# A four-layer graph network on one core: decoding and norm steps reordered in layer 0, inverse roots moved between layers 1 and 2

## The chip, the cores and the metric

The kernel runs on one core of a Trainium2 chip. The core has a matrix engine (TensorE, "PE" in the profile, with weight loads as "PEld"), three engines for elementwise work (VectorE or "DVE", ScalarE or "ACT", GpSimd or "POOL"), and SyncE ("SP"), which here only issues DMA transfers. Each engine runs its own instructions strictly in order, and engines wait for each other through semaphores. The metric is the time of one execution on the device in microseconds (us); lower is better.

## The reference

x has 2708 rows (nodes) of 512 features. adj is a 2708 x 2708 matrix that is almost empty: each entry is nonzero with probability 0.0015, plus the diagonal, with values in 0.05 to 1. Four layers follow one another, each of the form x = layernorm(x + layer(x, adj)):

```python
# layer 0
e2 = (adj @ x) * (diag + 1);        y = (x - e2) @ W + bias
# layer 1
h = x @ W_sa
scores = (h @ a_left)[:, None] + (h @ a_right)[None, :]
e = where(adj != 0, exp(-leaky_relu(scores, 0.01)), 0)
x_a = (e / (e.sum(1) + 1e-5)) @ h;  x_b = adj @ (x @ W_gcn) + b_gcn
y = sigmoid(gate_a * x_a + gate_b * x_b)      # gates: sigmoids of linear forms of adj @ x and x
# layer 2
mask = adj > 0;  inc = adj + mask / sqrt(mask.sum(1));  y = (inc @ x) / inc.sum(1)
# layer 3
A = adj + I;  d = A.sum(0) ** -0.5;  y = tanh((d[:, None] * A * d[None, :]) @ x @ W.T + b)
```

## The kernel before

**Lists instead of a dense matrix.** The 2708 rows are cut into NB = 24 blocks of R = 113 (the last has 109). For each block the kernel makes a list of up to 512 edges (four chunks of 128), and a product with adj becomes four products of a small matrix (128 edges by 113 rows) with 128 gathered rows of 512 features. The function `gather` (line 600) fetches those rows by four indirect DMAs that POOL issues; `aggregate` (L613) is the four products on PE. Layer 0 builds the lists as it goes; layers 1 to 3 use them again, gathering from tables in device memory that the layer before wrote.

**The order is written by hand** (`manual_schedule`): each engine executes its instructions in the order in which the code calls them. All direct loads and stores are issued from SP's single queue, in the order of the calls.

**Layer 0.** Blocks of 113 rows carry the aggregation, windows of 128 rows (KB = 22 of them) carry the products with the weights. Before the loop the first three blocks are searched, with some unread products (`keep_busy`, L797) placed on PE. Then 26 steps, k = 0 to 25, do the following, with m = k+2 the block whose list is decoded:

- `turn_x` transposes the last window's normalised rows (PE), `ranges`, `mark`, `fetch` (L901 to L913) decode block m's list: `starts` (L889 to L896: a PE product and three ACT instructions that make "ahead", "middle", "q") has been issued in the step before, `mark` compares q on DVE, and `fetch` is eight PE products.
- `project0` (o_l) multiplies a window by w0. In step k=1, two products `times_a` (L827), part of preparing layer 1's score weights, stand ahead of it; `score_rows` and `score_columns` copy and turn their result.
- `negatives` (L845) is an ACT pass over a whole adjacency block. `search` finds the eight largest values of one of four segments of a block, and their places (DVE, L858 and L860); after the fourth segment `count` (L872 to L882) sums up and the load of a later adjacency block is issued on SP. A step searches `parts` segments: 4, or 5 ahead of a step without a window, or fewer in and behind such a step.
- `pick` (L922 to L956) turns the fetched list into indices, row numbers and values, issues the gather of block m, and ends with an ACT instruction for `nvalue`. `values0(m)` makes the block's edge matrix with eight ACT instructions (L966, L967); `sums0(m)` (l0a) multiplies it in the step after.
- `load_window` loads a window of x on SP into one of two tiles `xw`, one step before `bias0` adds the bias to it (DVE, L990). `residual0` adds the projection (DVE L1000) and has three ACT instructions for the variance, the last a square root (L1009).
- `norm0` has a DVE reciprocal (L1017) and two ACT instructions (L1018, L1019) that write the normalised rows.
- `next0` (h) and `rest0` (hb) multiply the window before by layer 1's weights; `next0` ends in four ACT copies and the stores of `to_blocks`. `inputs0` (DVE, L979 to L984) and `turn_u` (L1064, L1073) prepare the next aggregated block.

Windows and blocks do not match, so steps 8 and 17 have no window ("bare"), and steps 9 and 18 follow them (`parts` = 3). The order at the end of a step before the change:

```python
                pick(m)
                own[m] = load_own(m)
...
                residual0(w)
...
            if w is not None:
                norm0(w)
            if wx is not None and not bare:
                next0(wx)
            if m < NB:
                values0(m)
            search(parts - 3)
            if k + 1 < NB:
                sums0(k + 1)
                inputs0(k + 1)
```

**Layer 1 and the way to layer 2.** In block i, `sums1` and `scored_sums1` are PE products, `gates1` and `gated1` work on the first, `both1`, `stats1` and `norm1` finish block i-1; `norm1` stores the block to table 1. `source_sums_in` brings column sums of adj into `deg` with a PE transpose and an ACT copy. `row_norms` (L1540 to L1545) makes inverse square roots of row counts with a power on POOL; `d_inv` (L1638) is another such power. `keep_warm(12)` (L1530) puts unread products on PE, and `spread_bias(b3_bc)` (L1504, L1505) broadcasts a bias row with a PE product and a DVE copy. Layer 2 starts with the gathers of blocks 0 and 1 from table 1 and with `incidence` (L1567, L1570), which makes the edge matrix `s_left` of a block on DVE.

**Layer 2 and the way to layer 3.** Per block: four gathers, four products (l2a), one unread product, statistics, and `norm2`, which writes the normalised rows `xr` and then `y`, which is xr scaled by d_inv, each with one ACT pass (L1689, L1693); y is stored to table 2, from which layer 3 gathers.

Of the kernel before, what the change touches and what calls it, by code (L numbers as in the profile page):

```python
# [447 lines left out]
def sparse_stack(  # L448
# [199 lines left out]
    with ExitStack() as phase:  # L648
# [106 lines left out]
        load_diagonal(0, 4, R)  # L755
        nc.sync.dma_start(out=w0_sb, in_=w0.rearrange("(b p) o -> p b o", p=P))
        own[1] = load_own(1)


        nc.gpsimd.iota(  # L760
# [385 lines left out]
        count(1)  # L1146
        starts(1)
        values0(0)
        keep_busy(2)
        find(2, (0,), places=False)  # L1150
        ranges(1)
        mark(1)
# [14 lines left out]
        load_adj(5)  # L1167
        count(2)
        sums0(0)
        starts(2)  # L1170
        gate_columns()
        turn_w(0)
# [33 lines left out]
        for k in range(NB + 2):  # L1206
            m = k + 2
            w, wx, rest = window_at.get(k), window_at.get(k - 1), window_at.get(k - 1)
            bare = 2 < k < NB and w is None
            after = 2 < k < NB and wx is None  # L1210
            parts = 4
            if any(t not in window_at for t in (k + 1, k + 2, k + 3)) and 2 < k < NB - 4:
                parts = 5
            if bare:
                parts, rest = 2, None
            if after:
                parts, rest = 3, window_at[k - 2]
            if wx is not None and k <= NB:
                turn_x(wx)
            if m < NB:  # L1220
                ranges(m)
                mark(m)
                fetch(m)
            if k == 1:
                times_a(2)
                times_a(3)
            if w is not None:
                project0(w)
            if k == 0:
                times_a(0)  # L1230
                turn_w(2)
            if unstored:
                store0(unstored.pop())
            if k + 3 < NB:
                negatives(k + 3)
            if k == 1:
                score_rows()
            search(1)
            if m < NB:
                pick(m)  # L1240
                own[m] = load_own(m)
            if w is not None:
                bias0(w)
            search(1)
            if w is not None:
                residual0(w)
            if k + 1 in window_at:
                load_window(window_at[k + 1])
            if parts > 2:
                search(1)  # L1250
            if w is not None:
                norm0(w)
            if wx is not None and not bare:
                next0(wx)
            if m < NB:
                values0(m)
            search(parts - 3)
            if k + 1 < NB:
                sums0(k + 1)
                inputs0(k + 1)  # L1260
            if k == 1:
                score_columns()
            if k + 2 == NB:
                worst = check_lists()
                for i in range(4):
# [232 lines left out]
    bg_bc = gpool.tile([P, D], FP, name="bg_bc")  # L1498
    nc.sync.dma_start(out=bg_bc[0:1, :], in_=b_gc[None, :])

    def spread_bias(t):
        ps = ps_sp.tile([P, 4, P], FP, tag="sp", name="bias_rows")
        ps = ps.rearrange("p k r -> p (k r)")
        nc.tensor.matmul(ps, lhsT=one_row, rhs=t[0:1, :], start=True, stop=True)  # L1504
        nc.vector.tensor_copy(t, ps)  # L1505
# [13 lines left out]
    def source_sums_in():  # L1519
        ps = ps_sp.tile([P, 4, P], FP, tag="sp", name="deg_s")  # L1520
        nc.tensor.transpose(ps[:R, 0, :NB], deg_r, ident[:NB, :NB])
        nc.scalar.copy(deg[:R, :], ps[:R, 0, :NB])

    def keep_warm(pool, tag, shape, n, cols=D):

# [11 lines left out]
    def row_norms(at):  # L1537
        n = at.stop - at.start

        nc.vector.tensor_scalar(  # L1540
            cnt[:, at], cnt[:, at], 2.0**23, 2.0**23, op0=ALU.add, op1=ALU.subtract
        )
        nc.vector.tensor_add(cnt[:, at], cnt[:, at], plus[:, at])
        nc.vector.tensor_scalar(inv_norm[:, at], cnt[:, at], 1e-24, None, op0=ALU.max)
        nc.gpsimd.tensor_tensor(  # L1545
            inv_norm[:, at], inv_norm[:, at], root.to_broadcast([P, n]), ALU.pow
        )

    row_in, inc2 = {}, {}

# [33 lines left out]
    for i in range(NB):  # L1584
# [41 lines left out]
    nc.vector.tensor_mul(plus, plus, inv_norm)  # L1626
    nc.vector.tensor_add(plus, plus, adiag)
    nc.vector.tensor_mul(cnt, cnt, inv_norm)
    nc.vector.tensor_add(rowsum, rowsum, cnt)
# [7 lines left out]
    nc.vector.tensor_add(d_inv, deg, zero)  # L1637
    nc.gpsimd.tensor_tensor(d_inv, d_inv, root.to_broadcast([P, NB]), ALU.pow)  # L1638
# [43 lines left out]
    def norm2(i):  # L1682
        r = rows(i)
        v, mv = v2.pop(i)
        nc.vector.reciprocal(mv[:r, 2:3], mv[:r, 2:3])
        nc.vector.tensor_scalar(
            mv[:r, 3:4], mv[:r, 0:1], mv[:r, 2:3], -1.0, op0=ALU.mult, op1=ALU.mult
        )
        nc.scalar.activation(  # L1689
            xr[:r, i, :], v[:r, :], AF.Identity, bias=mv[:r, 3:4], scale=mv[:r, 2:3]  # L1690
        )
        y = spool.tile([P, D], FP, tag="y", name=f"y2_{i}")
        nc.scalar.activation(y[:r, :], xr[:r, i, :], AF.Copy, scale=d_inv[:r, i : i + 1])  # L1693
        move_rows(r, lambda a, b: table[2][i * R + a : i * R + b, :], lambda a, b: y[a:b, :])

    own2(0)
# [149 lines left out]
```

## Time and profile before

| | us |
|---|---|
| median of 3 runs | 988.07 |
| lowest and highest run | 983.52, 988.93 |
| the profiled execution: its time | 1001.58 |
| its span, first to last instruction | 999.7 |

| busy in the profiled span | us | share |
|---|---|---|
| PE | 898.5 | 90% |
| PE weight loads | 498.5 | 50% |
| DVE | 685.7 | 69% |
| ACT | 527.9 | 53% |
| POOL | 472.4 | 47% |

The mean granted TensorE clock is 0.954. The stages, read from the timeline: the first 62 us are the start of layer 0, whose loop runs to about 419; layer 1 from there to 632, layer 2 from about 653 to 789, layer 3 from about 800 to the end. In a timeline each line gives start, length, engine, source line, operation, output<-inputs, shapes and count, and in brackets how long the engine had been idle before and what released it. A line of the source can be a helper's, so that one line stands for many tiles. One fp32 product appears as two PE records.

### The profile page before, as it was taken

The page shows a single profiled execution, that of the slowest core. Times are in us where ns is not written, and L with a number is a line of the kernel's source. Part 1 is how long each engine was busy: PE and PEld are TensorE (multiplying, and loading weights), DVE is VectorE, ACT ScalarE, POOL GpSimd, SP SyncE. Part 2 cuts the span into 40 slices and gives each one's busy share as a digit, 9 for nine tenths or more (in the row PEclk, how much of TensorE's full clock was granted, in tenths as well). Part 3 has the DMA queues.
Part 4 walks back from the last instruction along what each step waited for, and adds up shares of the span by engine and source line. Part 5 has one row for each costly group of instructions (what it writes and reads, how often), then busy time and mean ns, then how long its engine had stood idle before and what let it go on. Part 6 is the DMA issues. An engine that isn't in the chain of part 4 may idle for free.

```text
span 999.7 us, 11191 instructions
## 1 busy us (share of the span) xinstructions
PE 898.5 (90%) x2963; PEld 498.5 (50%) x2963; DVE 685.7 (69%) x1803; ACT 527.9 (53%) x1220; POOL 472.4 (47%) x538
## 2 busy tenths in 40 slices
PE   6789999899998999988888879887797889999994
PEld 2445656455654655466666667432332334444441
DVE  7877889787997743168888789586586525555543
ACT  5857677577677563357776667243354412222222
POOL 3322323323323220066666665576777375767640
PEclk8879999999999899989999999989898998999997
DMA  9976877787876444389999996266666464555531
GB/s 244 304 206 188 241 213 228 224 227 207 240 209 194 141 120 144 103 300 299 313 292 315 294 290 224 85 191 192 201 207 199 123 174 139 162 168 152 174 107 35
DMA packets 133516, 201.70 MB, mean 202 GB/s; under 512 B 82456, under 2 KB 82502, under 8 KB 133445
## 3 DMA queue, kind: packets, MB, share of 16 engines
q0 software_dynamic: 36864, 111.73, 37.4%
q1 hardware_dynamic: 96581, 89.18, 31.3%
q8 instruction: 26, 0.43, 0.2%
q14 instruction: 45, 0.37, 0.1%
HBM read 181.83 MB, written 27.80 MB: 210 GB/s over the span
## 4 chain that ended last, share of the span: by engine, by line
PE 66%; DVE 11%; DMA 9%; issue 4%; ACT 3%; POOL 3%; another core or an unknown queue 2%; SPq 1%; POOLq 0%; DVEq 0%; ACTq 0%
PE o_l L584 15%; PE l3a L613 9%; PE l2a L613 8%; PE hb L584 7%; PE h L584 7%; DMA gath<-table,source 7%; PE l0a L613 6%; PE unread L1530 3%; PE l1s L1407 3%; POOL gath L600 2%; PE fetched L913 2%; PE l1e L1417 2%; DVE where_all L860 2%; DMA gath<-in_x_dram 1%
## 5 line engine op out<-in xcount | busy, mean ns | idle before, releaser
L600 POOL DMA_INDIRECT gath<-table,source x288 | 314.6, 1093 | 164.9 <-issue 79.7
L600 POOL DMA_INDIRECT gath<-in_x_dram,source x96 | 97.8, 1019 | 233.7 <-issue 204.3
L1407 PE MATMUL l1s<-gath,s 128*113 128x256 f32 (+3 forms) x384 | 93.6, 398 | 23.9 <-DVE l1b L1437 23.4
L613 PE MATMUL l2a<-gath,s_left 128*113 128x512 f32 (+1 forms) x192 | 93.5, 629 | 3.5 <-DVE s_left L1570 2.0
L613 PE MATMUL l3a<-gath,s 128*113 128x512 f32 (+1 forms) x192 | 90.4, 614 | 3.6 <-DMA gath<-table,source 3.6
L1407 PEld LDWEIGHTS l1s<-gath,s 128*113 128x113 f32 (+1 forms) x384 | 68.7, 184 | 49.5 <-DVE l1b L1437 32.2
L1417 PE MATMUL l1e<-gath,e 128*113 128x257 f32 (+3 forms) x384 | 87.0, 379 | 0.2 <-issue 0.2
L613 PE MATMUL l0a<-gath,s 128*113 128x512 f32 (+1 forms) x192 | 86.9, 593 | 0.2 <-DMA gath<-in_x_dram,source 0.2
L584 PE MATMUL o_l<-shared,uT_l 128*113 128x512 f32 (+1 forms) x192 | 86.4, 592 | 0.7 <-ACT uT_l L577 0.7
L584 PE MATMUL hb<-w_gc_sb,uT_x 128*128 128x512 f32 (+1 forms) x176 | 83.3, 601 | 0.0
L584 PE MATMUL o_l<-w_sb,uw 128*128 128x512 f32 (+1 forms) x176 | 82.9, 615 | 0.2
L584 PE MATMUL h<-w_sa_sb,uT_x 128*128 128x259 f32 (+1 forms) x352 | 80.8, 382 | 0.0
L1417 PEld LDWEIGHTS l1e<-gath,e 128*113 128x113 f32 (+1 forms) x384 | 68.0, 177 | 15.7 <-issue 0.6
L584 PEld LDWEIGHTS h<-w_sa_sb,uT_x 128*128 128x128 f32 (+1 forms) x352 | 64.8, 185 | 19.8 <-issue 6.6
L1530 PE MATMUL unread<-bg_bc,ident 128*128 128x512 f32 x88 | 47.1, 655 | 21.9 <-remote 17.2
L1765 ACT ACTIVATE y<-l3v,mv_l 113x512 f32<-113x512 f32 (+1 forms) x24 | 19.5, 813 | 81.9 <-DVE mv_l L1761 74.4
L613 PEld LDWEIGHTS l2a<-gath,s_left 128*113 128x113 f32 (+1 forms) x192 | 34.4, 191 | 53.3 <-issue 44.5
L584 PEld LDWEIGHTS o_l<-shared,uT_l 128*113 128x113 f32 (+1 forms) x192 | 34.0, 177 | 48.7 <-issue 47.7
L1739 DVE SCALAR_TENSOR_TENSOR l3v<-o_l,d_inv,b_bc 113x512 f32<-113x512 f32 (+1 forms) x25 | 18.1, 729 | 58.5 <-PE o_l L584 55.1
L613 PEld LDWEIGHTS l3a<-gath,s 128*113 128x113 f32 (+1 forms) x192 | 33.3, 184 | 43.5 <-issue 39.4
L613 PEld LDWEIGHTS l0a<-gath,s 128*113 128x113 f32 (+1 forms) x192 | 33.5, 177 | 39.9 <-issue 35.3
L1294 DVE TENSOR_SCALAR s<-niota_r,nrow,edges 128x113 f32<-128x113 f32 x192 | 51.3, 342 | 0.0
(239 smaller groups left out, 1594.1 us busy)
## 6 DMA issues: line engine op xcount, KB each, us to landing
shared<-in_adj_dram SPq DMA_DIRECT2D x14, 1186.5 KB
table<-st SPq DMA_DIRECT2D x21, 514.5 KB
gath<-in_adj_dram SPq DMA_DIRECT2D x7, 1186.5 KB
shared<-table SPq DMA_DIRECT2D x16, 448.0 KB
gath<-in_x_dram SPq DMA_DIRECT2D x21, 256.0 KB
xi<-in_x_dram SPq DMA_DIRECT2D x23, 224.0 KB
table<-xr SPq DMA_DIRECT2D x23, 224.0 KB
table<-y SPq DMA_DIRECT2D x23, 224.0 KB
```

Of the source, the lines that this page charges most:

```text
L584: nc.tensor.matmul(o, lhsT=uT[:, f, :r], rhs=w[:, f, :], start=(f == 0), stop=(f == DB - 1))
L600: nc.gpsimd.indirect_dma_start(out=g[:, c, :n], out_offset=None, in_=src[:, :], in_offset=bass.IndirectOffsetOnAxis(ap=source[:, i, c : c ...
L613: nc.tensor.matmul(agg[:r, :], lhsT=s[:, c, :r], rhs=g[:, c, off : off + D], start=(c == 0), stop=(c == EC - 1),)
L860: nc.vector.max_index(out=where_all[:, i, g * 8 : (g + 1) * 8], in_max=top, in_values=seg)
L913: nc.tensor.matmul(t["fetched"][:, c, : 3 * NS], lhsT=t["q"][:, c * P : (c + 1) * P], rhs=rec_all[:, i].rearrange("p k s -> p (k s)"), sta ...
L1294: nc.vector.tensor_scalar(s[:, c, :], niota_r, nrow[:, i, c : c + 1], edges[:, i, c, 1:2], op0=ALU.is_equal, op1=ALU.mult,)
L1407: nc.tensor.matmul(sum_s[i][:r, k, : at.stop - at.start], lhsT=s[:, c, :r], rhs=g[:, c, at], start=(c == 0), stop=(c == EC - 1),)
L1417: nc.tensor.matmul(sum_e[i][:r, k, k : k + at.stop - at.start], lhsT=e[:, c, :r], rhs=g[:, c, at], start=(c == 0), stop=(c == EC - 1),)
L1530: nc.tensor.matmul(o[:, :cols], lhsT=ident, rhs=bg_bc[:, :cols], start=True, stop=True)
L1739: nc.vector.scalar_tensor_tensor(v[:r, at], o[:r, at], d_inv[:r, i : i + 1], b3_bc[:r, at], op0=ALU.mult, op1=ALU.add,)
L1765: nc.scalar.activation(y[:r, :], v[:r, :], AF.Identity, bias=mv[:r, 3:4], scale=mv[:r, 2:3])
```

## The change

In layer 0, the first two windows of x are loaded right behind block 1's own rows, ahead of adjacency block 3 and the later weights on SP's queue, and are no longer loaded in the loop. One of the two unread products before `fetch(1)` is taken away, and two are added behind `sums0(0)`. In a step, `project0` comes before `times_a(2)` and `times_a(3)`; `values0(m)` comes right behind `pick(m)` and `load_own(m)`, ahead of `bias0`; the last searches of a step are put together; `next0` comes before `norm0`, which is last. In step k=1 `score_rows` moves behind `values0`.

From layer 1 to layer 2: in the last iteration the statistics of block 22 come after `gated1(23)`; `source_sums_in` runs after the last `norm1`, and its copy is DVE's; the bias row's product goes out behind `both1(23)`, and the copy follows later; the incidence work of blocks 0 and 1 comes before the gathers; `d_inv` and the last two columns of `row_norms` use a square root on ACT and a reciprocal on DVE instead of POOL's power; the unread products fall from 12 to 8; the sums over `rowsum`, `plus` and `cnt` come behind the gathers' calls. In `norm2` of the last block y is made from v with a combined scale and bias, ahead of xr.

```diff
         own[1] = load_own(1)
+        load_window(0)
+        load_window(1)
...
-        keep_busy(2)
+        keep_busy(1)
         find(2, (0,), places=False)
...
         sums0(0)
+        keep_busy(2)
         starts(2)
...
+            if w is not None:
+                project0(w)
             if k == 1:
                 times_a(2)
                 times_a(3)
-            if w is not None:
-                project0(w)
...
-            if k == 1:
-                score_rows()
             search(1)
             if m < NB:
                 pick(m)
                 own[m] = load_own(m)
+                values0(m)
+            if k == 1:
+                score_rows()
...
-            if k + 1 in window_at:
+            if window_at.get(k + 1, 0) > 1:
                 load_window(window_at[k + 1])
-            if parts > 2:
-                search(1)
+            search(parts - 2)
+            if wx is not None and not bare:
+                next0(wx)
             if w is not None:
                 norm0(w)
-            if wx is not None and not bare:
-                next0(wx)
-            if m < NB:
-                values0(m)
-            search(parts - 3)
...
+    def spread_row(t, name):
+        ps = ps_sp.tile([P, 4, P], FP, tag="sp", name=f"rows_{name}")
+        spread_ps[name] = ps = ps.rearrange("p k r -> p (k r)")
+        nc.tensor.matmul(ps, lhsT=one_row, rhs=t[0:1, :], start=True, stop=True)
...
-        nc.gpsimd.tensor_tensor(
-            inv_norm[:, at], inv_norm[:, at], root.to_broadcast([P, n]), ALU.pow
-        )
+        if on_pool:
+            nc.gpsimd.tensor_tensor(
+                inv_norm[:, at], inv_norm[:, at], root.to_broadcast([P, n]), ALU.pow
+            )
+        else:
+            nc.scalar.sqrt(inv_norm[:, at], inv_norm[:, at])
+            nc.vector.reciprocal(inv_norm[:, at], inv_norm[:, at])
...
         if i + 1 == NB:
-            source_sums_in()
             turn_norm(0)
             turn_norm(1)
...
-        if i > 0:
+        if 0 < i < NB - 1:
             stats1(i - 1)
...
         if i + 1 < NB:
             mask1(i + 1)
+        else:
+            stats1(i - 1)
...
-    row_norms(slice(KB, NB))
     copy_norm(0)
     copy_norm(1)
-    keep_warm(ps_sp, "sp", [P, 4, P], 12)
+    keep_warm(ps_sp, "sp", [P, 4, P], 8)
     both1(NB - 1)
+    spread_row(b3_bc, "b3")
     stats1(NB - 1)
-    nc.vector.tensor_add(rowsum, rowsum, adiag)
...
     norm1(NB - 1)
+    deg_ps = source_sums_in()
+    inc_s = [values(0)]
+    incidence(0, inc_s[0])
+    inc_s.append(values(1))
+    incidence(1, inc_s[1])
+    nc.vector.tensor_copy(b3_bc, spread_ps["b3"])
+
+    nc.vector.tensor_copy(deg[:R, :], deg_ps[:R, 0, :NB])
...
-    nc.gpsimd.tensor_tensor(d_inv, d_inv, root.to_broadcast([P, NB]), ALU.pow)
-    spread_bias(b3_bc)
+    nc.scalar.sqrt(d_inv, d_inv)
+    row_norms(slice(KB, NB), False)
...
     for i in range(2):
         gather(gath[i], i, table[1], D)
-        incidence(i, values(i))
+    nc.vector.tensor_add(rowsum, rowsum, adiag)
...
+    nc.vector.reciprocal(d_inv, d_inv)
     nc.vector.reciprocal(rowsum, rowsum)
...
+        if i + 1 == NB:
+
+            di = d_inv[:r, i : i + 1]
+            nc.vector.tensor_mul(mv[:r, 0:2], mv[:r, 2:4], di.to_broadcast([r, 2]))
+            nc.scalar.activation(
+                y[:r, :], v[:r, :], AF.Identity, bias=mv[:r, 1:2], scale=mv[:r, 0:1]
+            )
```

More of the change, by code (lines that the diff above doesn't have):

```diff
@@ L1499, in sparse_stack @@
     nc.sync.dma_start(out=bg_bc[0:1, :], in_=b_gc[None, :])
+    spread_ps = {}
+    def spread_row(t, name):
+        ps = ps_sp.tile([P, 4, P], FP, tag="sp", name=f"rows_{name}")
+        spread_ps[name] = ps = ps.rearrange("p k r -> p (k r)")
+        nc.tensor.matmul(ps, lhsT=one_row, rhs=t[0:1, :], start=True, stop=True)
     def spread_bias(t):
@@ L1521, in source_sums_in @@
         nc.tensor.transpose(ps[:R, 0, :NB], deg_r, ident[:NB, :NB])
-        nc.scalar.copy(deg[:R, :], ps[:R, 0, :NB])
+        return ps
     def keep_warm(pool, tag, shape, n, cols=D):
@@ L1535, in sparse_stack, with row_norms @@
     nc.vector.tensor_scalar(plus, adiag, 0.0, None, op0=ALU.is_gt)
-    def row_norms(at):
+    def row_norms(at, on_pool=True):
         n = at.stop - at.start
@@ L1618, in sparse_stack @@
             row_norms(slice(0, KB))
-    row_norms(slice(KB, NB))
     copy_norm(0)
     copy_norm(1)
-    keep_warm(ps_sp, "sp", [P, 4, P], 12)
+    keep_warm(ps_sp, "sp", [P, 4, P], 8)
     both1(NB - 1)
+    spread_row(b3_bc, "b3")
     stats1(NB - 1)
-    nc.vector.tensor_add(rowsum, rowsum, adiag)
[L1626 to L1629, printed above, removed]
-    norm1(NB - 1)
+    norm1(NB - 1)
+    deg_ps = source_sums_in()
[5 more added lines that the diff above has]
+    nc.vector.tensor_copy(deg[:R, :], deg_ps[:R, 0, :NB])
     nc.vector.tensor_add(deg, deg, adiag)
@@ L1649, in sparse_stack @@
         gather(gath[i], i, table[1], D)
-        incidence(i, values(i))
+    nc.vector.tensor_add(rowsum, rowsum, adiag)
+    nc.vector.tensor_mul(plus, plus, inv_norm)
+    nc.vector.tensor_add(plus, plus, adiag)
+    nc.vector.tensor_mul(cnt, cnt, inv_norm)
+    nc.vector.tensor_add(rowsum, rowsum, cnt)
+    nc.vector.reciprocal(d_inv, d_inv)
     nc.vector.reciprocal(rowsum, rowsum)
@@ L1688, in norm2 @@
         )
+        y = spool.tile([P, D], FP, tag="y", name=f"y2_{i}")
+        if i + 1 == NB:
[4 more added lines that the diff above has]
+            )
         nc.scalar.activation(
@@ L1691, in norm2 @@
         )
-        y = spool.tile([P, D], FP, tag="y", name=f"y2_{i}")
-        nc.scalar.activation(y[:r, :], xr[:r, i, :], AF.Copy, scale=d_inv[:r, i : i + 1])
+        if i + 1 < NB:
+            nc.scalar.activation(y[:r, :], xr[:r, i, :], AF.Copy, scale=d_inv[:r, i : i + 1])
         move_rows(r, lambda a, b: table[2][i * R + a : i * R + b, :], lambda a, b: y[a:b, :])
```

## The prediction

> **What bounds the kernel now.** I read the chain of waits first, over the whole span: it names an engine for each stretch. Then the busy time by stretch, to separate full stages from stages with holes, then the timeline around each hole that a changed line touches.
>
> Busy time by stretch; columns are the stretch, its length, then busy time (and instructions) of PE, PE weight loads, DVE, ACT and POOL, granted TensorE clock, DMA share, GB/s:
>
> ```profile
> 160.00:190.00 30.00, 26.32 (x106) 15.37 (x105) 22.73 (x63) 21.97 (x54) 8.83 (x9) 1.00 0.76 218
> 190.00:298.00 108.00, 108.00 (x390) 63.75 (x389) 92.96 (x246) 75.62 (x192) 31.13 (x36) 1.00 0.81 222
> 298.00:326.00 28.00, 24.28 (x96) 14.25 (x95) 20.86 (x59) 19.98 (x48) 9.12 (x10) 0.96 0.58 174
> ```
>
> Layer 0's ordinary steps leave PE nothing idle (108.00 of 108), so moving ACT or DVE work there is worth nothing by itself. Time can come only from holes, and two lie at 160 to 190 and 298 to 326, one step after each step without a window (k=9 and k=18). In order of time, the first and its twin's end:
>
> ```profile
> 180.42 0.20 ACT L1005 ACTIVATE st_l<-st_l 128x1 f32<-128x1 f32 x1 [5.21 <-DVE l0v L1000]
> ...
> 182.76 0.29 ACT L1018 ACTIVATE st_l<-st_l 128x1 f32<-128x1 f32 x1 [0.96 <-DVE st_l L1017]
> ...
> 183.81 0.37 ACT L966 ACTIVATE away<-iota_r,nrow 128x113 f32<-128x113 f32 x1
> ...
> 186.99 0.24 ACT L892 ACTIVATE ahead<-fetched,totals 128x1 f32<-128x1 f32 x1
> ...
> 188.61 1.13 PE L913 MATMUL fetched<-rec_all,q 128*128 128x96 f32 x8 [2.68 <-DVE q L908]
> ...
> 324.44 2.02 PE L913 MATMUL fetched<-rec_all,q 128*128 128x96 f32 x8 [2.69 <-DVE q L908]
> ```
>
> ACT idles 5.21 us, then does norm0, then all eight instructions of values0 (183.81 to 187.08), and only then "ahead" and "q", on which the mark on DVE and PE's fetch wait: 2.68 us. values0's inputs were ready at 175.4.
>
> At the start the chain runs through DVE's list search, with these waits:
>
> ```profile
> 27.36 0.29 DVE L922 TENSOR_TENSOR mine<-fetched,lane 128x128 f32<-128x128 f32 x1 [1.54 <-PE fetched L913]
> ...
> 39.17 0.29 DVE L922 TENSOR_TENSOR mine<-fetched,lane 128x128 f32<-128x128 f32 x1 [0.86 <-PE fetched L913]
> ...
> 54.73 0.69 DVE L990 TENSOR_TENSOR gath<-gath,gath 128x512 f32<-128x512 f32 x1 [1.86 <-DMA gath<-in_x_dram]
> ```
>
> The chain of waits (start, length, work) has the two times_a products ahead of the first o_l:
>
> ```profile
> 50.54 3.50 PE w_a L827 x4
> 54.04 3.65 PE o_l L584 x8
> ```
>
> Between layers 1 and 2 the timeline shows POOL's power before the gathers, DVE waiting for a bias row behind 12 keep-warm products, and PE for DVE:
>
> ```profile
> 641.63 4.17 POOL L1638 TENSOR_TENSOR d_inv<-d_inv,root 128x24 f32<-128x24 f32 x1 [1.06 <-DVE d_inv L1637]
> ...
> 645.98 1.17 POOL L600 DMA_INDIRECT gath<-table,source  x1 [0.17 <-issue]
> ...
> 649.66 0.69 DVE L1505 COPY b_bc<-bias_rows 128x512 f32<-128x512 f32 x1 [8.11 <-PE bias_rows L1504]
> ...
> 652.75 6.31 PE L613 MATMUL l2a<-gath,s_left 128*113 128x512 f32 x8 [2.03 <-DVE s_left L1570]
> ```
>
> Between layers 2 and 3 two ACT passes stand before the store that the gathers wait for (793.37 to 795.67 in the chain of waits):
>
> ```profile
> 791.77 0.81 ACT L1689 ACTIVATE xr<-l2v,mv_l 109x512 f32<-109x512 f32 x1 [0.48 <-DVE mv_l L1686]
> 792.62 0.72 ACT L1693 ACTIVATE y<-xr,d_inv 109x512 f32<-109x512 f32 x1
> ```
>
> **What the Trainium skill says.** "TensorE: Matmul & The Clock Gate", Part 1 (The HAM clock gate): after about 3.4 us of little work PE falls to half clock, and needs about 3.4 us of work to come back; the window runs freely, so the moment varies. The trace agrees: fp32 512-column records take 0.43 us warm; after two equal 2.68 us holes only the second (clock 0.50 from 324 to 330) paid. fetch plus o_l took 2.02+5.47 = 7.49 us there, 1.13+3.46 = 4.59 after the first: 2.90 more. "ScalarE activation tables: per-element evaluation and per-set limits", What a function is on this engine: functions of different sets are one table load of 1283 ns apart. The trace has one of 1.28 us at 660.33 before layer 2's first Sqrt. "DMA: Bandwidth & Descriptors", Issuing engines are not separate DMA queues: all issuers share the 16 engines. So tiles loaded earlier push back other loads (DMA share over 1.0 from 20 to 48 us).
>
> **Part by part**, against the profiled execution (span 999.7, 1001.58 in all).
>
> *Start, until the first q (0 to 49 us).* One dummy product fewer ahead of fetch(1): two took 3.62 us cold, so fetch is 1.8 earlier, and DVE's 1.54 wait goes. Two dummy products behind sums0(0) fill a 2.98 us hole on PE before starts(2); warm they take 1.7. Warm, the 8 weight-transpose records, tr and fetch cost 1.0+0.4+0.9 instead of 2.03+0.75+1.69, and the 0.86 wait goes too: 2.4. Against this, two x tiles (0.52 MB) pass ahead of adjacency 3, w_sa and w_gc on SP's queue. Summing that queue's bytes per us from 18 us, w0, x, adjacency 3 and w_sa (3.55 MB) are through at 31.8; at 0.38 MB/us the tiles add 1.4: 33.2, plus a delay to report taken as 1 (the small store at 793.72 takes 1.95 whole). PE wants w_sa at 32.6 then, so it waits until some 34.1 (34.67 now). If still warm, fetch ends at 36.4 instead of 39.15, before DVE asks (36.8); if cold, at 38.6. Bounds -0.6 and -2.4; ACT's run of values0(1), negatives, values0(2), q follows tr closely, so I take -1.9.
>
> *Step k=1.* The x tile is there: DVE's 1.86 wait goes, with two searches behind it. project0 before times_a: in the cold stretch (4 records of 0.87, then 4 of 0.43) o_l ends 5.2 us after fetch instead of 7.15, -1.9. score_rows on ACT now waits for times_a (+1.7 behind o_l) with residual0's statistics and the 1.28 table load behind it, but the reciprocal comes after the searches, which cover all but 0.4. Next late is l0a(2), about 59.5, inputs0 to 61.7 if the first part brought 1.5; now it ends at 65.67. So 65.67-1.5-61.7: -2.5 for this step, bounds -1.5 and -3. Start in all: -4.4.
>
> *Ordinary steps.* values0 (8 instructions, 3.4 us of ACT) now runs while ACT waited for residual0; norm0 stands behind next0's four copies and all searches. Its deadline is turn_x. In the step from 147 to 163, five searches, the reciprocal moves from 155.99 to about 159.3, the scaled pass ends at 160.6, turn_x starts at 163.18: 2.6 us to spare. inputs0 on DVE keeps its place. Nothing, for PE hides it.
>
> *k=9 and k=18.* values0 falls into the 5.21 (5.75) us in which ACT idles for residual0. Then q follows norm0 at 184.3, mark follows inputs0 at 185.0 to 185.5, fetch follows turn_x at 185.9: the hole of 2.68 shrinks to nothing, twice -2.7. What stays is bias0's wait for its window (2.17, 2.72): that load is not moved. Without the second hole the cold stretch should go: -2.9, bounds 0 and -2.9.
>
> *Layer 0's end.* norm0(21) behind next0's copies: Identity ends 410.0 against turn_x at 409.94: +0.1.
>
> *Layer 1 to 2.* POOL loses the 4.17 us power; the gathers then wait for the last table store. Issued at 641.70, it lands about 2.3 later, as the same pair does at 793.37 to 795.67: 644.0. In the last iteration the deg copy no longer blocks ACT's gate (1.1 us) and row_norms (0.5) leaves DVE ahead of both1, while stats1 with POOL's power moves in between: about -0.45 on that store. POOL's first gather comes 1.08 after landing (795.67 to 796.75): 644.6 against 645.98, -1.35; bounds 0 and -2.2. The table load falls after norm1's pass and before d_inv, hidden. The incidence work, now before the gathers land, takes l2a(0) off DVE: it starts with gather 0, near 648.2 (3.45 us after issue, as at 796.75 to 800.24), instead of 652.75. That is not the gain: layer 2 follows POOL, at 1.3 us a gather 5.2 a block against PE's 4.39, so only -1.35 survives. Fewer keep-warm products end at 644.6; PE idles 2.5 and starts cold as before.
>
> *Layer 2 to 3.* y comes from v with a combined scale: one small DVE product (0.2) for one ACT pass (0.72): -0.55. The pass for xr hides behind the gathers.
>
> Sum: -4.4 -5.4 -2.9 +0.1 -1.35 -0.55 = -14.5 of 999.7. The profile is 11.6 us longer than the median 988.07; PE's waits for an unknown queue in layer 2 (17.2 us in all) may be the cause, which nothing here shows. The clock depends on the window's phase, so on the median I count half of it: -13.05, **975**.
>
> **Rivals.**
> - *The start keeps nothing*: w_sa arrives still later, PE is cold again, the tiles' time is paid back; the clock saving and layer 2's are absent too. For: saturated DMA. Against: three waits that go. Left: 5.4+0.55-0.1 = 5.9, **982**.
> - *The holes close up again*: at k=9 the fetch meets another late input, such as the window tile or the gather (0.18 at 314.85). For: DVE's 2.17 wait remains. Against: it lies before 182.57, and all after it is counted. Only 2 us: **986**.
> - *Slower*: norm0 late in every step. Its pass now needs last search, reciprocal, two ACT passes; the deadline breaks if the last search ends after 161.8 in the 147 step (159.3 expected). One us beyond costs 1 us in some 20 steps: **995**. For: DVE is full in five-search steps. Against: 2.6 us of slack, 4 in four-search steps.
> - *More*: shorter stalls in layer 2 as well, **966**.
>
> **How the numbers follow.** Chances: forecast 0.62 (its own range 969 to 981), start lost 0.18, closed again 0.07, slower 0.06, more 0.07. The range 966 to 984 leaves out the second and third rival and some tail. About 0.5% (5 us) is what this measurement can tell from none: below 983.1 lie the forecast, most of the first rival and the fourth (0.84); within it the rest of the first and the second (0.10); above, 0.06.
>
> **What would show it.** Right: no wait of fetch for q in k=9 and k=18; values0 beginning right behind nvalue; first ordinary step some 4 us earlier; POOL's gathers of layer 2 starting a us after the store. Wrong: PE waiting for w_sa past 35 us, turn_x waiting for ACT in ordinary steps, or clock 0.50 near k=18 again.

## The result, and the profile after

The kernel after takes 971.1 us (median of four runs, 970.3 to 972.5) against 987.9 for the kernel before: ratio 0.9849, 95% interval 0.9826 to 0.9872. The forecast was 975. In a later comparison on another chip it was 970.31 against 984.16, ratio 0.9849 again (0.9819 to 0.9879).

The spans of the two first profiles, 999.7 and 970.3, differ by more than the medians. The excess lies in layers 2 and 3, where the execution of before that was profiled had stalls of some 5 us that its repetition below doesn't have. (Time against time that execution stood 13.5 us above the median, 1001.58 against 988.07; the prediction's 11.6 sets its span against the median. No term rests on it.) I therefore compare stages by intervals between the same two instructions, over several profiles.

**The holes.** Busy time by stretch, kernel after; columns as before (stretch, length, PE, weight loads, DVE, ACT, POOL, clock, DMA share, GB/s):

```profile
160.00:190.00 30.00, 29.20 (x113) 16.48 (x112) 25.62 (x73) 23.96 (x55) 8.99 (x10) 1.00 0.83 240
190.00:298.00 108.00, 108.00 (x403) 64.68 (x402) 92.75 (x245) 74.69 (x192) 30.89 (x36) 1.00 0.80 217
298.00:326.00 28.00, 27.38 (x103) 16.07 (x102) 24.58 (x67) 23.76 (x58) 12.12 (x14) 1.00 0.76 224
```

PE stands still for 0.8 us at k=9 and 0.6 us at k=18, and the ordinary steps between are full, as they were. The timeline of ACT in step k=9, kernel after:

```profile
175.21 0.22 ACT L958 ACTIVATE nvalue<-edges 128x4 f32<-128x4 f32 x1
175.67 0.39 ACT L968 ACTIVATE away<-iota_r,nrow 128x113 f32<-128x113 f32 x1 [0.24 <-DVE nrow L955]
...
178.49 0.48 ACT L969 ACTIVATE s<-away,edges,nvalue 128x113 f32<-128x113 f32 x1
180.67 0.20 ACT L1007 ACTIVATE st_l<-st_l 128x1 f32<-128x1 f32 x1 [1.70 <-DVE l0v L1002]
...
183.34 0.81 ACT L1021 ACTIVATE gath<-l0v,st_l 128x512 f32<-128x512 f32 x1
184.06 0.24 ACT L894 ACTIVATE ahead<-fetched,totals 128x1 f32<-128x1 f32 x1
...
184.38 0.72 ACT L898 ACTIVATE q<-gath,middle 128x512 f32<-128x512 f32 x1
```

values0 (175.67 to 178.97) stands right behind nvalue, inside the time that ACT spends waiting for residual0. When the normalizing pass ends (184.15), "ahead" and "q" are next. The timeline of PE in the same two steps, kernel after:

```profile
186.02 1.03 PE L915 MATMUL fetched<-rec_all,q 128*128 128x96 f32 x8
186.88 3.62 PE L584 MATMUL o_l<-w_sb,uw 128*128 128x512 f32 x8
...
318.23 1.03 PE L915 MATMUL fetched<-rec_all,q 128*128 128x96 f32 x8
319.10 3.62 PE L584 MATMUL o_l<-w_sb,uw 128*128 128x512 f32 x8
```

No wait for q stands behind either fetch, and all four run at the full clock.

**The start.** The chain of waits of the kernel after (start, length, work):

```profile
19.91 9.21 SPq L677
29.16 0.38 SPq L508
...
30.47 7.41 DMA w_rows<-in_L_gnn_a_sa_dram
38.01 0.27 PE w_rows_t L807
```

and two lines of its timeline of DVE, the fetches of lists 1 and 2:

```profile
26.34 0.29 DVE L924 TENSOR_TENSOR mine<-fetched,lane 128x128 f32<-128x128 f32 x1 [0.40 <-PE fetched L915]
...
42.73 0.29 DVE L924 TENSOR_TENSOR mine<-fetched,lane 128x128 f32<-128x128 f32 x1 [5.44 <-PE fetched L915]
```

Two lines of SP's timeline, kernel before:

```profile
18.43 6.34 SPq L677 DMA_DIRECT2D gath<-in_adj_dram  x1
24.81 0.39 SPq L508 DMA_DIRECT2D w_sa_sb<-in_L_gnn_W_sa_dram  x1
```

The first wait fell from 1.54 to 0.40 as forecast. But SP was held for 9.21 us in the tail of adjacency 3 (6.34 before), w_sa was issued at 29.16 instead of 24.81, and the second list's fetch ended at 42.71 instead of 39.15: DVE waits 5.44 us.

**Layer 1 to 2 and 2 to 3.** The timelines of POOL, PE and ACT, kernel after:

```profile
618.08 3.86 POOL L1553 TENSOR_TENSOR inv_norm<-inv_norm,root 128x22 f32<-128x22 f32 x1 [2.13 <-DVE rec L1452]
...
635.09 1.37 POOL L600 DMA_INDIRECT gath<-table,source  x1 [4.56 <-PE unread L1537]
...
638.93 1.11 PE L613 MATMUL l2a<-gath,s_left 128*113 128x512 f32 x2 [1.64 <-DMA gath<-table,source]
...
771.36 0.81 ACT L1713 ACTIVATE y<-l2v,mv_l 109x512 f32<-109x512 f32 x1 [0.68 <-DVE mv_l L1712]
772.08 0.80 ACT L1716 ACTIVATE xr<-l2v,mv_l 109x512 f32<-109x512 f32 x1
```

The 128x22 power in POOL's timeline, kernel before:

```profile
627.30 3.86 POOL L1545 TENSOR_TENSOR inv_norm<-inv_norm,root 128x22 f32<-128x22 f32 x1 [2.12 <-DVE rec L1452]
```

From the start of the 128x22 power to the first gather of layer 2 it is 17.01 us; before it was 18.68 (627.30 to 645.98). The 128x24 power is gone. The first l2a starts 3.84 us after the first gather, where it took 6.77, but from the first gather to the last l2a it is 133.5 us in after and 133.6 in before's repetition: the earlier start of the products is not the gain, as the prediction said. y now leaves ACT ahead of xr.

### The profile page after: what moved, and what is told of

The parts are those of the page before. It is cut to its first block, busy times and chain, and to the rows that moved or that the text cites. A ratio compares the mean times of both kernels' runs of the same rounds, so it can differ in the third digit from the quotient of the medians.

```text
span 970.3 us, 11188 instructions
## 1 busy us (share of the span) xinstructions
PE 890.4 (92%) x2957; PEld 492.3 (51%) x2957; DVE 686.6 (71%) x1807; ACT 528.0 (54%) x1221; POOL 466.6 (48%) x536
## 4 chain that ended last, share of the span: by engine, by line
PE 58%; DMA 19%; DVE 8%; issue 5%; POOL 5%; SPq 2%; ACT 2%; POOLq 0%; DVEq 0%; ACTq 0%
DMA gath<-table,source 16%; PE o_l L584 15%; PE l3a L613 9%; PE hb L584 7%; PE h L584 7%; PE l0a L613 6%; POOL gath L600 4%; PE l2a L613 3%; PE l1s L1407 2%; PE fetched L915 2%; PE unread L1537 2%; SPq L677 2%; DMA gath<-in_x_dram 1%; PE l1e L1417 1%; PE tr_l L1066 1%
## 5 line engine op out<-in xcount | busy, mean ns | idle before, releaser
L1407 PE MATMUL l1s<-gath,s 128*113 128x256 f32 (+3 forms) x384 | 98.3, 412 | 21.1 <-DVE l1b L1437 20.6
L613 PE MATMUL l2a<-gath,s_left 128*113 128x512 f32 (+1 forms) x192 | 96.8, 619 | 16.4 <-DMA gath<-table,source 16.2
L1407 PEld LDWEIGHTS l1s<-gath,s 128*113 128x113 f32 (+1 forms) x384 | 71.5, 191 | 48.2 <-DVE l1b L1437 28.1
L613 PE MATMUL l3a<-gath,s 128*113 128x512 f32 (+1 forms) x192 | 88.3, 602 | 3.1 <-DMA gath<-table,source 3.1
L613 PEld LDWEIGHTS l2a<-gath,s_left 128*113 128x113 f32 (+1 forms) x192 | 29.6, 179 | 73.1 <-DMA gath<-table,source 56.2
L862 DVE FIND_INDEX8 where_all<-rec_all,shared 128x8 uint32<-128x678 f32 (+1 forms) x64 | 51.2, 800 | 0.0
## 6 DMA issues: line engine op xcount, KB each, us to landing
shared<-in_adj_dram SPq DMA_DIRECT2D x14, 1186.5 KB
gath<-in_adj_dram SPq DMA_DIRECT2D x7, 1186.5 KB
```

Source lines behind the costliest of these rows:

```text
L613: nc.tensor.matmul(agg[:r, :], lhsT=s[:, c, :r], rhs=g[:, c, off : off + D], start=(c == 0), stop=(c == EC - 1),)
L862: nc.vector.max_index(out=where_all[:, i, g * 8 : (g + 1) * 8], in_max=top, in_values=seg)
L1407: nc.tensor.matmul(sum_s[i][:r, k, : at.stop - at.start], lhsT=s[:, c, :r], rhs=g[:, c, at], start=(c == 0), stop=(c == EC - 1),)
```

## The experiments

The runs came in three groups, each on a chip of its own with the kernel before beside it: 984.06, 984.16 and 1001.61 us. The first group is before_again, b_steps, x_in_loop and x_behind_wgc; the second after_again, w_ahead, values_back and b_late; the third values_only, norm_back, b_start and w_ahead_warm. The two first profiles belong to the comparison above. Ratios are against before in the same group. The table gives, for each profile, where h of the first ordinary step starts, the time from h to h across k=9 and across k=18 (an ordinary step is 15.7), from POOL's 128x22 power to layer 2's first gather, and from the end of the last l2a to the first l3a. The last column is the ratio with its interval.

| kernel | first h | k=9 | k=18 | 1 to 2 | 2 to 3 | ratio |
|---|---|---|---|---|---|---|
| before, first profile | 73.5 | 25.0 | 28.4 | 18.7 | 11.0 | |
| before_again | 74.0 | 27.4 | 29.1 | 18.7 | 11.0 | |
| after, first profile | 73.7 | 22.1 | 21.9 | 17.0 | 10.5 | 0.985 (0.983-0.987) |
| after_again | 71.5 | 23.5 | 22.6 | 17.2 | 10.5 | 0.985 (0.982-0.988) |
| b_steps | 70.7 | 23.4 | 21.8 | 18.7 | 11.1 | 0.988 (0.984-0.991) |
| x_in_loop | 72.4 | 23.6 | 23.4 | 17.2 | 10.5 | 0.986 (0.983-0.990) |
| x_behind_wgc | 70.0 | 22.4 | 22.1 | 17.0 | 10.4 | 0.984 (0.980-0.987) |
| w_ahead | 69.4 | 22.0 | 21.5 | 17.4 | 10.5 | 0.981 (0.978-0.984) |
| b_late | 72.5 | 30.0 | 24.1 | 17.2 | 10.5 | 0.997 (0.996-0.999) |
| values_back | 76.8 | 25.8 | 22.3 | 17.2 | 10.5 | 1.011 (1.008-1.014) |
| values_only | 74.0 | 21.7 | 20.6 | 18.7 | 11.0 | 0.993 (0.991-0.996) |
| norm_back | 78.0 | 21.9 | 21.1 | 17.2 | 10.5 | 0.992 (0.990-0.995) |
| b_start | 77.1 | 26.6 | 23.7 | 18.7 | 11.0 | 1.003 (1.001-1.005) |
| w_ahead_warm | 67.7 | 21.7 | 21.1 | 18.2 | 10.4 | 0.985 (0.982-0.988) |

**before_again**, the kernel before unchanged.

> The kernel before, unchanged, profiled once more. Theory 1: the four stalls of about 5 us on TensorE in layer 2 of the first profile (waits for an unknown queue) belong to that execution alone. Then the span is 986 to 990 us, and from POOL's first gather of layer 2 to the last product l2a it takes about 133 us as in the kernel after (142.6 in the first profile). Rival: the kernel before stalls there in every execution, 140 us or more again, and the change cured it.

It took 984.65 us in its one execution, span 982.9. From the first gather to the end of the last l2a it is 133.6 us (647.04 to 780.64), against 133.5 in after. Waits of engines in layers 2 and 3 of the first profile of before, the releaser unknown:

```profile
PE unread L1530 <- remote: 17.2, 4, 5.3
DVE l2v L1671 <- remote: 17.9, 3, 7.2
```

Neither is in the second profile. Theory 1 holds: the change didn't cure these stalls. In the third group every profile has such waits (PE on the unread products: 12.8 to 18.3 us), and two of those four, norm_back and w_ahead_warm, carry the changed layers 2 and 3.

**b_steps**, the order inside the steps alone: after's loop with the tiles loaded as before, before's code elsewhere.

```diff
+            if w is not None:
+                project0(w)          # ahead of times_a
...
+                values0(m)           # right behind pick and load_own
+            if k == 1:
+                score_rows()
...
+            search(parts - 2)
+            if wx is not None and not bare:
+                next0(wx)
             if w is not None:
                 norm0(w)
```

> The kernel before, with the changed order inside the steps of layer 0 alone (values0 right behind pick, project0 ahead of times_a, score_rows later, next0 and all searches ahead of norm0); tiles, dummy products and all after layer 0 as before. Theory 1: the holes at k=9 and k=18 go (2.7 us each), the half clock behind the second with them (0 to 2.9), and step k=1 gives 1 to 2.5: in all 978 to 981. Rival: the order alone closes the holes only with an earlier start, under 3 us: 985 or more.

972.61 us against 984.06: 11.5 less, above what theory 1 expected. Both holes closed, and the first h came 3.3 us earlier than in before_again, although the tile was still late in step k=1 (DVE waited 1.65 us for it).

**values_only**, one edit on the kernel before: values0 moved from behind next0 to behind `own[m] = load_own(m)`.

> The kernel before with one edit: values0 right behind pick. Theory 1 (that edit alone closes the two holes): no wait of fetch for q at k=9 and k=18, gaps there 22 to 24 us instead of 25 to 30, step k=1 unchanged; about 7 to 9 us less than before, a ratio of 0.991 to 0.993. Rival (norm0 still ahead of next0 keeps q late): a wait of 1 us or more stays at both places, a ratio of 0.995 or more.

994.78 against 1001.61. Theory 1: the start is unchanged (74.0) and both holes close as far as in any kernel. PE's timeline in k=9 and k=18, values_only:

```profile
186.00 1.03 PE L913 MATMUL fetched<-rec_all,q 128*128 128x96 f32 x8
186.87 3.62 PE L584 MATMUL o_l<-w_sb,uw 128*128 128x512 f32 x8
...
316.96 1.03 PE L913 MATMUL fetched<-rec_all,q 128*128 128x96 f32 x8
317.83 3.62 PE L584 MATMUL o_l<-w_sb,uw 128*128 128x512 f32 x8
```

**norm_back**: the kernel after with norm0 again ahead of next0 and of the last searches.

```diff
-            search(parts - 2)
+            if parts > 2:
+                search(1)
+            if w is not None:
+                norm0(w)
             if wx is not None and not bare:
                 next0(wx)
-            if w is not None:
-                norm0(w)
+            search(parts - 3)
```

> The kernel after with norm0 back ahead of next0 and of the later searches, values0 left early. Theory 1 (with values0 early nothing on ACT is pressed, and norm0's place is free within its slack): gaps as after, 22 to 23.5, in all 970 to 972. Rival (norm0's late place is needed, since its wait for residual0 holds next0's copies and with them PE's h): ordinary steps longer than 15.7 us or gaps of 24 and more, 975 or more.

Gaps 21.9 and 21.1, every ordinary step 15.7 to 15.9: by these intervals the late place of norm0 brings nothing. The time, 992.3, fits neither theory's number, because this chip's times are higher throughout and after itself was not run there; the ratio, 0.992 against 0.985 on the other chips, I can't split. Its first h at 78.0 is 4 to 7 us later than after's, with the same wait for the weight rows (5.12 us on DVE) and twice as much half clock: from 51.9 to 58.8 (o_l 5.62 us) and from 69.0 to 75.8, each time about 3.4 us in after's first profile.

**values_back**: the kernel after with values0 back behind norm0 and next0.

```diff
                 own[m] = load_own(m)
-                values0(m)
...
                 norm0(w)
+            if m < NB:
+                values0(m)
```

> The kernel after with values0 alone put back behind norm0 and next0, everything else as after. Theory 1 (values0 on ACT ahead of q is what makes the holes): waits of fetch for q at k=9 and k=18 of 2.7 us or more come back, since norm0 and next0 now stand ahead of it as well; gaps there 25 us or more instead of 22; in all 977 to 982. Rival (next0 ahead of norm0, or the searches, closed the holes): gaps stay at 22 to 23, 970 to 973.

996.89 us, 12.7 slower than before and far outside both expectations. The gap at k=9 came back (25.8), that at k=18 didn't reach the 25 of theory 1 (22.3). The waits of PE from 75 to 430 us, values_back (engine, tile, line, what it waited for, us in all, times, longest):

```profile
PE fetched L915 <- DVE q L910: 14.5, 9, 2.7
```

Its timelines of ACT and PE in an ordinary step:

```profile
132.43 0.81 ACT L1021 ACTIVATE gath<-l0v,st_l 128x512 f32<-128x512 f32 x1
133.15 0.37 ACT L968 ACTIVATE away<-iota_r,nrow 128x113 f32<-128x113 f32 x1
...
135.94 0.48 ACT L969 ACTIVATE s<-away,edges,nvalue 128x113 f32<-128x113 f32 x1
136.33 0.24 ACT L894 ACTIVATE ahead<-fetched,totals 128x1 f32<-128x1 f32 x1
...
137.95 1.13 PE L915 MATMUL fetched<-rec_all,q 128*128 128x96 f32 x8 [2.00 <-DVE q L910]
```

Now the late normalizing pass, then values0, then q stand in a row, in ordinary steps too: those run 15.7 to 19.7 us, and from the first h to the last layer 0 takes 352.1 us instead of 329.3. The transposes of `turn_x` (tr_x) don't wait: PE has no wait of its own for them in layer 0 (their weight load has one, of 0.8 us). So the two moves are not independent: norm0 can stand last only because values0 has left that place.

**b_start**: the kernel before with the start part alone.

```diff
         own[1] = load_own(1)
+        load_window(0)
+        load_window(1)
...
-        keep_busy(2)
+        keep_busy(1)
...
         sums0(0)
+        keep_busy(2)
...
-            if k + 1 in window_at:
+            if window_at.get(k + 1, 0) > 1:
```

> The kernel before with the start part alone: two x tiles ahead of adjacency 3, one dummy product moved. Theory 1 (the tiles cost at the weight rows about what they bring at the tile wait of step k=1): w_sa leaves SP at 27 to 29 us, DVE waits about 5 us for the second list's fetch, no tile wait, h of the first ordinary step at 73 to 76 as against 74.0; ratio 0.998 to 1.002. Rival (the forecast's own -1.9 for this part): h near 72, a ratio of 0.997 or less by the start alone.

1005.37 against 1001.61, ratio 1.003: this part alone costs, a little more than theory 1 gave it. Its first h, 77.1, is 3 us behind values_only's, which has the old start in the same group. The timelines of SP and DVE, b_start:

```profile
18.17 0.97 SPq L569 DMA_DIRECT2D gath<-in_x_dram  x2
...
19.81 9.40 SPq L677 DMA_DIRECT2D gath<-in_adj_dram  x1
...
43.62 0.29 DVE L924 TENSOR_TENSOR mine<-fetched,lane 128x128 f32<-128x128 f32 x1 [6.51 <-PE fetched L915]
```

The same picture as in after: 9.40 us in adjacency 3's tail, then w_sa at 29.26, then 6.51 us of DVE waiting.

**x_in_loop** takes the tiles' two early loads out of after again (they are loaded in the loop, as before); **x_behind_wgc** issues them behind w_gc.

> The kernel after, with the first two x tiles loaded inside the loop again, as before. Theory 1 (the two tiles ahead of adjacency 3 hold up w_sa and the weight rows on SP's queue): w_sa is issued near 25 us instead of 29, the second list's fetch ends near 38.5 instead of 42.7, the wait for the tile in step k=1 (1.9 us) comes back; the first ordinary step's h starts near 71.5 to 72 instead of 73.9; in all 969 to 970. Rival (something else sets the start, the tiles only a part): w_sa near 29 again, h at 74 or later, 971 to 973.

> The kernel after, with the two early x tiles issued behind w_gc instead of ahead of adjacency 3. Theory 1: w_sa leaves SP near 25 us, fetch of list 2 ends near 38.5, no wait for the tile in step k=1, h of the first ordinary step at 70 to 71, in all 967 to 968. Rival: adjacency 3 itself, or the dummy products moved, set the time of that fetch: h at 73 to 74, 971.

x_in_loop: w_sa left SP at 24.13, DVE had the second list at 36.90 without a wait, and in step k=1 waited for the tile's landing at 54.9; first h at 72.4. The two effects are there, and they nearly cancel in the first h; the time, 972.56 (967.06 to 976.09), can't be told from after's. x_behind_wgc: w_sa at 25.47, no tile wait, first h at 70.0, 968.93 us. But the rows were still late (DVE waited 3.37 us), since SP stood 3.01 us in the first of them. In x_in_loop, where the same loads stand ahead of it, that was 0.91; why isn't shown:

```profile
18.98 6.45 SPq L677 DMA_DIRECT2D gath<-in_adj_dram  x1
...
25.90 3.01 SPq L1136 DMA_DIRECT2D w_rows<-in_L_gnn_Wa_dram  x1
```

**w_ahead**: w_sa and the weight rows ahead of adjacency 3, the tiles behind w_gc; the rest as after.

```diff
+        w_sa_sb = load_w(w_sa, "w_sa_sb", first, more=6)
+        for k, src in enumerate((wa, wb, a_sa)):
+            ...
         load_adj(3)
-        w_sa_sb = load_w(w_sa, "w_sa_sb", first, more=6)
-        for k, src in enumerate((wa, wb, a_sa)):
-            ...
         w_gc_sb = load_w(w_gc, "w_gc_sb", first)
+        load_window(0)
+        load_window(1)
```

> The kernel after with w_sa and the weight rows issued ahead of adjacency 3, and the two early x tiles behind w_gc. Theory 1 (bytes ahead of the weight rows on SP's queue set the second list's fetch, the tile's own landing sets step k=1): w_sa leaves SP near 18.5 us, PE does not wait for the rows, DVE has the second list near 37 and the tile needs no wait, h of the first ordinary step at 66 to 67, in all 964 to 966. Rival (adjacency 3, now later by about 1 MB or some 2.7 us, holds DVE's search of list 3 instead): h at 69 to 71, in all 968 to 970.

966.74 us (963.5 to 968.58) beside after's 970.31 (969.36 to 971.77) on the same chip: the lowest ratio to before here, 0.981, though its interval overlaps that of x_behind_wgc. The timelines of SP, DVE and PE, w_ahead:

```profile
22.60 7.89 SPq L677 DMA_DIRECT2D gath<-in_adj_dram  x1
...
37.26 0.27 DVE L922 TENSOR_TENSOR mine<-fetched,lane 128x128 f32<-128x128 f32 x1
...
47.72 1.89 PE L913 MATMUL fetched<-rec_all,q 128*128 128x96 f32 x8
49.40 5.33 PE L584 MATMUL o_l<-w_sb,uw 128*128 128x512 f32 x8
```

w_sa leaves SP at 18.01, and the list is there at 37.26 without a wait. h at 69.4 is the rival's number, but not by its mechanism: adjacency 3 doesn't hold the search up (DVE waits for no load there). Of the 5 us won, 2 to 4 arrive at the first h. PE waits 1.15 and 2.12 us around the starts of list 3, the clock is halved from 46.0 to 52.8, and fetch and o_l take 7.0 us together, 6.3 and 6.0 in after's two profiles.

**w_ahead_warm** adds `keep_busy(3)` behind turn_w(2) and `keep_busy(1)` behind turn_w(3) in step k=0.

> The kernel with w_sa and rows ahead of adjacency 3 and tiles behind w_gc, plus four dummy products on PE in step k=0 (three behind turn_w(2), one behind turn_w(3)), where PE stood idle and went to half clock. Theory 1: tr_l, fetch and o_l of step k=1 run warm (0.58, 0.87 and 3.46 us instead of 0.99, 1.68 and 5.12), h of the first ordinary step at 65 to 67 instead of 69.4, in all 963 to 964. Rival (the dummies delay the starts that DVE waits for, or the next step waits for DVE instead): h at 68 to 70, 966 to 968.

Step k=1 runs at full clock, but the dummies put the starts of list 3 from 44.44 to 46.55, and the next step runs at half clock instead. PE's timeline, w_ahead_warm:

```profile
46.55 0.28 PE L889 MATMUL fetched<-totals,under 128*128 128x1 f32 x2
...
49.47 3.62 PE L584 MATMUL o_l<-w_sb,uw 128*128 128x512 f32 x8
...
61.03 0.98 PE L1064 MATMUL tr_l<-ident,l0u 113*128 113x113 f32 x4 [1.86 <-DVE rec_all L901]
...
62.66 1.75 PE L913 MATMUL fetched<-rec_all,q 128*128 128x96 f32 x8
```

First h at 67.7, between the theories' numbers; the ratio, 0.985 on the third chip, doesn't show it ahead of w_ahead. Inconclusive.

**b_late**: the kernel before with everything behind layer 0 as after.

> The kernel before with the parts behind layer 0 alone (root on ACT and later norms between layer 1 and layer 2, the last block's combined scale between layer 2 and layer 3). Theory 1: from the start of POOL's first power to its first gather of layer 2 17.0 instead of 18.7 us, from the last l2a's end to the first l3a 10.5 instead of 11.0; 2.2 us in all, so a ratio near 0.998. Rival: fewer stalls in layer 2 too, 4 us or more, a ratio of 0.996 or less.

981.88 against 984.16: 2.3 us, as theory 1 says, with both intervals as expected.

**after_again**, after unchanged beside these.

> The kernel after, unchanged, on the same chip as the next three. Theory 1: gaps from h to h around k=9 and k=18 near 22 us again, first ordinary h near 73.7, span 968 to 972, POOL's first power of layer 1's end to its first gather 17.0 us. Rival: the gaps follow the clock's phase and one of them is 23 to 27 this time.

970.31 us, the gaps 23.5 and 22.6. The first lies in the rival's range, but the clock was full there. First h at 71.5: the clock stayed full from 55.4, so that fetch and o_l of the next step, k=2, took 1.03 and 3.62 us, where after's first profile has 1.86 and 3.82.

To the first gather it is 17.2. In after the profile names the keep-warm products as what released that gather: they end at 635.07, it starts at 635.09. This run rules them out. Its chain of waits, and one line of its timeline of PE:

```profile
631.64 2.58 DMA table<-xr
...
635.23 3.47 DMA gath<-table,source
```

```profile
626.21 10.13 PE L1537 MATMUL unread<-bg_bc,ident 128*128 128x512 f32 x16 [2.75 <-ACT row_in L1571]
```

The last table store lands at 634.22 and the gather follows 1.0 us later, while the products run on to 636.34.

## Why the prediction was right, and where it wasn't

**The start (-4.4) is the term that failed**: by the first h it was worth +0.2 and -2.0 us in after's two profiles, against a mean of 73.5 in the four with before's start and project0 behind times_a (72.5 to 74.0); norm_back, with the same start, even lies at 78.0. Its first part (-1.9) had the wrong sign: alone it costs 2.8 us by the ratio of b_start (interval 0.9 to 4.6), 3 us at the first h. The step was "at 0.38 MB/us the tiles add 1.4: 33.2, plus a delay": a sum of bytes for when w_sa would be through. The runs show something else: SP itself is held while it issues adjacency 3's tail, for 9.2 us with the tiles ahead (6.9 to 9.4 in four more profiles) and 5.4 to 6.5 without. The loads behind it aren't in the queue at all until then: the last weight row left SP at 29.9 to 30.6 in the five profiles with the tiles ahead, and at 25.9 to 26.4 in six of the seven with the old order up to w_gc (29.3 in x_behind_wgc). It then lands some 7.5 us after its issue (7.41 in after, 7.60 in after_again). PE got the rows at 38.01, not at 34.1. "PE waiting for w_sa past 35" was named as the sign of an error, and came, for the rows behind w_sa. What holds SP stays open.

**Step k=1 (-2.5)** was about rightly sized, but it comes by the order more than by the tile: b_steps, where the tile is late, gets 3.3 against before_again, one profile each, with the 1.5 us between old starts as noise. In after the late weight rows use it up. The rival "the start keeps nothing" was right on its own point; its 982 was wrong, since it took the clock saving and layer 2's part away as well.

**The holes (-2.7 each)** closed by the mechanism given: values0 into ACT's idle time ahead of residual0, q right behind norm0. The fetch of k=9 was forecast at 185.9 and came at 186.02; the start, which that number leaves as it was, lay within 0.2 us of before's in that profile. values_only shows that this one line does it. **The clock term (-2.9, half of it on the median)** was sized too small. It was put on k=18 alone. With before's order in these steps (before, before_again, b_late, b_start: eight holes), PE ran the following products at half clock in five, now at k=9, now at k=18; fetch and o_l together then took 1.7 to 3.2 us more than the 4.59 of a pair at full clock, 12.7 in all, or 3.2 for a kernel. PE's timeline in k=18, before_again:

```profile
327.71 2.02 PE L913 MATMUL fetched<-rec_all,q 128*128 128x96 f32 x8 [2.71 <-DVE q L908]
329.53 6.00 PE L584 MATMUL o_l<-w_sb,uw 128*128 128x512 f32 x8
```

In none of the nine profiles with values0 early did it happen there. "TensorE: Matmul & The Clock Gate", Part 1 (The HAM clock gate) of the Trainium skill says that the window runs freely; the changing place agrees. Holes and clock together: k=9 plus k=18 took 53.5 us on average in the four profiles with before's order, 45.0 in after and after_again: -8.5 for -6.85 forecast on the median, and near the 8.6 of two holes and the 3.2 together.

**Ordinary steps at nothing**: right, 15.7 us before and after. The slack of norm0 held: in the step from 147 its pass ends at 160.76 in after (160.6 forecast), and turn_x starts at 163.40. values_back shows what the late norm0 stands on: with values0 behind it, q comes late and fetch waits in ordinary steps too. That is a path the prediction didn't price. The slow rival had turn_x waiting for ACT, which didn't come; that values_back's 996.9 lies beside its 995 is chance. That norm0 and its searches were moved brought nothing by norm_back's intervals, as priced.

**Layer 1 to 2 (-1.35)**: -1.67 by the interval above, by the mechanism given: the first gather now follows the landing of the last table store, 1.0 us later in after_again (1.08 forecast). **Layer 2 to 3 (-0.55)**: 11.0 to 10.5.

The sum measured by stages is about -1.1 (the mean start of two profiles each) -8.5 -1.6 -0.5 = -11.7, against 13.85 between the medians on one chip and 16.8 in the first comparison. The rest of 2 to 5 us I can't place: the stretch from the last h to POOL's 128x22 power alone took 212.5 us in before_again, 215.0 in before and 219.7 in b_start, with the same code there. That the forecast came within 4 us is therefore in part luck: the start gave some 3 us less than forecast, the holes with the clock 1.7 more, and the unplaced rest covers what is missing.

## What to carry to other kernels

On an engine that works in order, work whose inputs are ready goes into the wait that the engine has anyway, ahead of the instruction that waits; one such line closed both holes by itself (values_only, 6.8 us). Two moves that are harmless together can be costly alone, so undo them one by one. When a load is moved ahead on a full queue, ask when the issuing engine gets to the loads behind it, not only how many bytes stand ahead; here the weights that PE waits for had to go first (w_ahead).

## What was not expected of the hardware

- A load's issue can hold SP for 5.4 to 9.4 us (the tail of an adjacency block, 8.8 KB, behind 1186.5 KB in rows of 452 bytes). The same order doesn't always hold it equally: up to w_gc x_in_loop and x_behind_wgc issue the same loads, yet their last weight row left SP at 25.86 and 29.29.
- From the first gather to the last l2a, layer 2 took 133 to 135 us in nine profiles, and 142 to 146 in the four of the third group and in the first profile of before. In these five alone PE and DVE wait there for something that the profile doesn't name. Whether the chip decides it isn't shown.
- A hole of 2.7 us on PE was followed by half clock five times in eight. "TensorE: Matmul & The Clock Gate", Part 1 of the Trainium skill, speaks of an idle window of about 3.4 us; here less was enough. In all five PE had also waited 0.5 us or more within the 12 us before; the two holes without such a wait kept the full clock, and one with it did too.
